# Two items of the first expert worked on inside the attention's schedule, in an adaLN block with a dense-gated mixture of experts

## The chip, the cores and the metric

The kernel runs on one core of a Trainium2 chip. The core has five engines with instruction queues of their own: TensorE (PE in the profile; its weight loads are PEld), VectorE (DVE), ScalarE (ACT), GpSimd (POOL) and SyncE (SP), and 16 DMA engines that they share. The metric is the device time of one execution in microseconds (us); lower is better. A time is the median of several executions without the profiler.

## The reference

The input `x` is 2 sequences of 2,048 tokens with 256 features, in float32. The block is an attention half and an expert half, each with a layer norm, a scale, a shift and a gate that come from a conditioning vector:

```python
h = _layernorm(x) * (1 + ca) + sa
x = x + ga * attention(h)          # 2 heads of 128, one shared key and value head, rope, causal
h = _layernorm(x) * (1 + cb) + sb
gate = softmax(h @ Wg + bg)        # 8 experts
w = relu(gate - 0.125 * sigmoid(h @ Wt + bt)); w = w / (sum(w) or 1)
x = x + gb * sum_e w[:, e] * (gelu(h @ W1[e] + b1[e]) @ W2[e] + b2[e])
```

An expert has a weight above zero for only a part of the tokens, and the kernel computes it for those alone. From the reference's inputs expert 0 has 2,640 of the 4,096 tokens, experts 1 to 7 have 2,609, 2,370, 2,710, 2,418, 2,886, 3,614 and 1,806.

## The kernel before, in words

**The attention half** is a list of steps that a small planner (`Plan`, L40) puts in order when the program is built. Each step has an engine, an assumed cost, the steps it follows, the buffers it takes and gives (`room`, L184), a `late` time for what still has to land, and a rank. At every moment a free engine takes the ready step of lowest rank; the instructions are then emitted in that order, so that an engine's queue is fixed and an instruction that waits holds all behind it. The waits themselves come from the data. Work goes by tiles of 128 tokens (`tile_steps`, L398): load, norm, q, k and v, scores (L498), exponentials (L524), transposes of the probabilities (`turn_p`, L568), `pav` (L580), projection (`proj`, L615), residual, the second norm (`hx`, L638), a copy of its 16-bit halves to `feats` in DRAM (L648), transposes (`turn_h`, L662) and the gate's logits (L671). For groups of tiles `gate_steps` (L689) computes the weights and, for each token and expert, the place in that expert's list; `scatter` (L778) writes the entries of expert 0 to `lists[0]` in DRAM, one indirect DMA for a tile. An entry holds two weights (one per sequence, one of them zero), and the token's number. The tiles of the two sequences alternate; 24 of the 32 tiles come in groups of four, the last four one by one. `total` (L810) writes the counts that the expert half's loops read.

**The expert half** (`experts`, L832) is one critical section with a program for each engine, loops over run-time counts and semaphores by hand. An item is 256 tokens of one expert, in two columns of 128. SP reads an expert's list into `sheets[e]` (L887); POOL copies the item's token numbers (L1100), gathers their rows of `feats` into `xr` by two indirect DMAs (L1055), SP transposes `xr` into `xp` (L895), DVE joins the halves into `xT` (L994), PE does `h = W1 xT` and `y = W2 g` (L944, L935), ACT the gelu between (L970), DVE the bias and the gate (L1025, L1037), and POOL adds the two columns to `out` by two indirect DMAs (L1089). During expert e's first items POOL also writes the list of expert e+1, four tiles with each item (`write`, L1065). If an expert's last item holds at most 128 tokens, it is worked on as one column in a branch of its own (L869).

In the order of time between the halves: the last scatter of expert 0's list lands; all engines pass the barrier of the critical section; SP reads the list (`read(0)`, L903); POOL fetches item 0 (L1119), clears `yo`, writes the first four tiles of list 1 (L1125) and adds zeros to `out` (L1127), since the loop's `add` lies two items behind its fetch; DVE joins `xT` and PE begins. At the end POOL adds the last item's two columns (`add(t0 + 1)`, L1162); where that item has one column, the second one is zeros.

Of the kernel before, what the change touches and what calls it, by code (L numbers as in the profile page):

```python
# [1 line left out]

# [9 lines left out]
F32 = mybir.dt.float32  # L12
BF16 = mybir.dt.bfloat16
I32 = mybir.dt.int32
# [6 lines left out]
P = 128  # L21
# [10 lines left out]
NW = 4  # L32
NP = NTOK // P // NW
SC = 512
EPS = 1e-5
# [63 lines left out]
def adaln_block_kernel(ctx, tc, x, wqkvT, woT, wgt, bgt, w1, b1T, w2, b2, cT, wmod, rope, out):  # L99
# [17 lines left out]


    nc = tc.nc
    PSUM = bass.MemoryType.PSUM  # L120
# [7 lines left out]

    counts = const.tile([P, 3 * E], I32, name="counts")

# [7 lines left out]
    weights = []  # L138

    with tc.manual_schedule():  # L140
        attention(
            tc, x, wqkvT, woT, wgt, bgt, w1, b1T, w2, b2, cT, wmod, rope, out, ident, counts,
            b1_sb, b2_bc, gb_bc, lists, feats, place, entry, weights, wpool,
        )

# [3 lines left out]
    for e in range(RES, E):  # L149
# [4 lines left out]
    xp = ep.tile([P, CI * 2 * KD, P], U16, name="xp")  # L154
    xT = ep.tile([P, KD, TI], F32, name="xT")
    gs = [ep.tile([P, TI], F32, name=f"g{z}") for z in range(4)]
    gate = ep.tile([P, CI, D], F32, name="gate")
    part = ep.tile([P, CI, D], F32, name="part")
    yb = ep.tile([P, CI, D], F32, name="yb")
    yo = ep.tile([P, CI, D], F32, name="yo")  # L160
    sheets = [ep.tile([P, NTOK // P, ENT], F32, name=f"sheet_{e}") for e in range(E)]
    at = ep.tile([P, CI], I32, name="at")
    mcur = ep.tile([P, CI, ENT], F32, name="mcur")
    who = ep.tile([P, CI], I32, name="who")
    to = ep.tile([P, NW], I32, name="to")
# [4 lines left out]
        tc, nc, lists, feats, out.rearrange("b t d -> (b t) d"), counts, ident, b1_sb, b2_bc,  # L170
        gb_bc, w1, w2, weights, xr, xp, xT, gs, gate, part, yb, yo, sheets, at, mcur, who, to, new, place,
        entry, hs, ys,
    )


def attention(
    tc, x, wqkvT, woT, wgt, bgt, w1, b1T, w2, b2, cT, wmod, rope, out, ident, counts,
    b1_sb, b2_bc, gb_bc, lists, feats, place, entry, weights, wpool,
):

    nc = tc.nc
    PSUM = bass.MemoryType.PSUM
    ctx = ExitStack()
    room = {"ps": 6, "pav": 2, "x": 9, "s": 18, "pT": 3, "hx": 4, "hp": 3, "qT": 3, "big": 3, "xn": 3,  # L184
            "hT": 2, "hT2": 2, "aT": 2, "g_sb": 1, "sign": 1, "size": 1, "ga": 1}
# [26 lines left out]

    back = const.tile([P, 2, NTOK // P], F32, name="back")
    limits = const.tile([P, NP], F32, name="limits")
    wqkv_sb = const.tile([P, KD, 4 * HS], F32, name="wqkv_sb")
# [24 lines left out]
    )  # L240
    nc.vector.tensor_copy(back[:, 0, :], ids)
    nc.gpsimd.memset(entry, 0.0)
    nc.gpsimd.tensor_copy(
# [5 lines left out]
    def load(dst, src, kb, rank=first, **how):  # L249
# [13 lines left out]
        for q in range(NT // 4)  # L263
    ]
    l_m1 = load(wm_1, wm[:, :, 2 * D :], 1024, rank=0.5)
    l_wo = load(wo_sb, woT.rearrange("(h p) d -> p h d", p=P), 256, rank=0.5)
    l_wg = load(wgt_sb, wgt.rearrange("(k p) e -> p k e", p=P), 9, rank=0.5)
    l_bg = load(bgt_sb, bgt.partition_broadcast(P), 5, rank=0.5)
    load(b1_sb, b1T, 32, rank=6.0)
    load(  # L270
        b2_bc.rearrange("p e d -> p (e d)"), b2.rearrange("e d -> (e d)").partition_broadcast(P),
# [91 lines left out]

    prev = []
    for e in range(RES):
        prev = [
            plan.add(
                "SP", 11.0, lambda e=e: load_expert(e), after=m_wo + m_mod + [m_T] + prev, late=2.0,
                rank=8.0 + 4 * e,
            )  # L370
        ]


# [24 lines left out]
    def tile_steps(b, i, r, group, g):  # L398
# [161 lines left out]
        def dens():  # L560
            st["rd"] = little([P, NH], "rd", u)
            nc.vector.reduce_sum(st["rd"], st["den"][:, :, :nch], axis=AX.X)
            nc.vector.reciprocal(st["rd"], st["rd"])

        n_d = add("DVE", 0.32, dens, list(n_e.values()))

# [122 lines left out]
    def gate_steps(b, i0, m, q, group, after):  # L689
# [30 lines left out]
        def weigh():  # L720
            st["before"] = before = little([P, 4, E], "before", u, BF16)
            if befores:
                nc.vector.tensor_copy(before[:, 0, :], befores[-1])
            else:
                nc.vector.memset(before[:, 0, :], 0.0)
            befores.append(little([P, E], "next", u, BF16))
            ge, thr = st["ge"][:, :m], st["thr"][:, :m]
            tot = little([P, 4], "tot", u)[:, :m]
            nc.vector.reduce_sum(tot, ge, axis=AX.X)
            nc.vector.reciprocal(tot, tot)  # L730
            nc.vector.tensor_tensor(ge, ge, wide(tot), ALU.mult)
            nc.vector.tensor_scalar(thr, thr, 0.0625, 0.0625, ALU.mult, ALU.add)
            nc.vector.tensor_tensor(ge, ge, wide(thr), ALU.subtract)


            st["on"] = on = little([P, 4, E], "on", u, BF16)
            nc.vector.tensor_scalar(on[:, :m], ge, 0.0, None, ALU.is_gt)
            for j in range(m):
                dst = st["before"][:, j + 1, :] if j + 1 < m else befores[-1]
                nc.vector.tensor_tensor(dst, st["before"][:, j, :], on[:, j, :], ALU.add)  # L740
# [52 lines left out]
        for j in range(m):  # L793
            plan.add(
                "POOL", 1.27, lambda j=j: scatter(j), after=[n], rank=r + 10.0, late=3.0
            )
        return n

    order_w = []
    groups = [(0, 4), (1, 4)] * 3 + [(0, 2), (1, 2), (0, 1), (1, 1), (0, 1), (1, 1)]  # L800
    begun, q = [0] * B, 0
    for b, m in groups:
# [4 lines left out]
        begun[b] += m  # L807
        q += m

    def total():  # L810
# [3 lines left out]
        nc.vector.tensor_copy(n[:, 1:], pn[:, 1:E])  # L814
        nc.vector.tensor_scalar(n[:, :1], pn[:, :1], 1.0, None, ALU.max)
        nc.vector.tensor_copy(counts[:, :E], n)

        more = little([P, E, NP], "more", "")
        nc.vector.tensor_tensor(
# [4 lines left out]
        nc.vector.tensor_copy(counts[:, E : 2 * E], n)  # L824
        nc.vector.tensor_scalar(counts[:, 2 * E :], n, -1.0, float(NP), ALU.mult, ALU.add)

    plan.add("PE", 0.2, total, after=[last], take=["ps"], give=["ps"], rank=q)
    plan.run()
# [3 lines left out]
def experts(  # L832
    tc, nc, lists, feats, rows, counts, ident, b1_sb, b2_bc, gb_bc, w1, w2, weights, xr, xp, xT, gs,
    gate, part, yb, yo, sheets, at, mcur, who, to, new, place, entry, hs, ys,
):
# [3 lines left out]
    LAG = 2  # L839
    ENGINES = (ET.PE, ET.Activation, ET.DVE, ET.Pool, ET.SP)  # L840

# [13 lines left out]
    def items_of(eng, n):  # L855
        return eng.snap((n + (TI - 1)) >> 8, min_val=0, max_val=NTOK // TI)

    def items(eng, n, body, begin=None):
# [16 lines left out]
    with tc.tile_critical():  # L875
# [7 lines left out]
        with nc.Block() as block:  # L883

            @block.sync
            def _(sync):
                def read(e):  # L887

                    if e > 0:
                        sync.wait_ge(sem["written"], (e * NP + 1) * (16 * NW))  # L890
                    sync.dma_start(
# [3 lines left out]
                def turn(t):  # L895

                    sync.wait_ge(sem["loaded"], t * (16 * CI) + 16 * CI)
                    sync.sem_inc(sem["paused"], 1)
# [3 lines left out]

                read(0)  # L903
                turn(0)
                done, t0 = 1, 0
# [57 lines left out]
            def _(act):  # L963
# [11 lines left out]
                def begin(e):  # L975

                    if e == 0:

                        act.wait_ge(sem["planed"], 16)
                    if e + RES < E:  # L980
# [12 lines left out]
            def _(dve):  # L993
# [10 lines left out]
                def item(e, i, t, parts):  # L1004
                    dve.tensor_copy(mcur, sheets[e][:, ds(i * CI, CI), :]).then_inc(
                        sem["copied"], 1
# [34 lines left out]
                def begin(e):  # L1041
                    dve.wait_ge(sem["read"], 16 * e + 16)

                n = [count(dve, e, NTOK) for e in range(E)]
                dve.sem_inc(sem["ready"], 1)
                ready(0)
                items(dve, n, item, begin)

            @block.gpsimd
            def _(pool):  # L1050
# [34 lines left out]

                def scatter(t):

                    for c in range(CI):
                        pool.indirect_dma_start(  # L1089
# [8 lines left out]
                def fetch(index, t):  # L1098
# [3 lines left out]
                    ).then_inc(sem["indexed"], 1)  # L1102
                    wait("indexed", t + 1)
                    gather(t)

                def add(t):
                    wait("added", t * (16 * CI))
                    wait("biased", t + 1)
                    scatter(t)

                def item(e, i, t, also=None):
                    wait("planed", t * 16)
                    fetch(sheets[e][:, ds(i * CI, CI), 2:3], t)
                    if also is not None:
                        also()
                    add(t)

                wait("read", 16)
                fetch(sheets[0][:, 0:CI, 2:3], 0)  # L1119
                pool.memset(yo, 0.0).then_inc(sem["biased"], 1)  # L1120
                pool.iota(
                    who, pattern=[[P, CI]], base=0, channel_multiplier=1
                ).then_inc(sem["biased"], 1)
                wait("biased", 2)
                write(1, 0, 0)  # L1125
                wait("planed", 16)
                scatter(0)  # L1127
                done, t0 = 1, 0
                for e in range(E):
                    many = items_of(pool, count(pool, e, NTOK))  # L1130
                    if e > 0:
                        wait("read", 16 * e + 16)
                    if e == E - 1:
# [27 lines left out]
                add(t0)  # L1161
                add(t0 + 1)  # L1162

# [49 lines left out]
```

## Time and profile before

| what | us |
|---|---|
| median of 3 executions without the profiler (1703.48 to 1704.22) | 1704.15 |
| the profiled execution, its own time | 1719.86 |
| its span, first to last instruction | 1718.0 |
| PE busy in the span (95%) | 1635.1 |
| of it the items' matmuls, L944 and L935 | 675.1 and 673.5 |
| POOL busy (50%) | 863.9 |
| DVE busy (39%), ACT busy (40%) | 678.2, 684.3 |

The profile is of one execution, which is 15.7 us above the median; differences of instants are read from it. PE executes two instructions for each float32 matmul of the code, so an item of 16 + 16 matmuls shows 64 instructions; the 2,816 of L944 are 88 items. Busy time of an engine is not a bound by itself: whether an idle stretch of PE costs time depends on where it lies.

### The profile page before, as it was taken

Reading aid. Unit: us, or ns where it says so; the run is one execution under the profiler, and the core shown is the slowest. Engines: PE = TensorE matmul, PEld = TensorE weight load, DVE = VectorE, ACT = ScalarE, POOL = GpSimd, SP = SyncE. Lnnn points to the kernel's source line nnn. Section 1 sums busy time; section 2 is a strip of 40 time slices with the busy share of each in tenths; the row PEclk is TensorE's granted clock in tenths of the full one; section 3 lists DMA queues with packets and bytes.
Section 4 is the critical chain, followed back from the end, with each engine's and each line's share of the span. In section 5 each row is a group of like instructions: output and inputs, shape, how many; then the busy total and the mean of one; then the engine's idle time right before and its main releaser. Section 6 shows DMA issues by size and latency. Waiting matters only on the chain.

```text
span 1718.0 us, 26912 instructions
## 1 busy us (share of the span) xinstructions
PE 1635.1 (95%) x7665; PEld 1355.1 (79%) x7665; DVE 678.2 (39%) x2215; ACT 684.3 (40%) x1475; POOL 863.9 (50%) x1000
## 2 busy tenths in 40 slices
PE   6999999999949999999999999999999999999996
PEld 3666666677638888888888888888788888888885
DVE  5876766655632332223222232232222232222322
ACT  2444555555523333333333333333333343333432
POOL 2332222111127767765775774676677467744443
PEclk9999999999979999999999999999999999999998
DMA  6210100000014334334434533433433333333333
GB/s 224 84 38 26 35 22 26 25 14 13 16 26 106 59 69 105 59 65 81 85 57 61 105 59 66 99 62 57 104 60 59 61 56 61 60 58 58 64 58 47
DMA packets 166476, 106.98 MB, mean 62 GB/s; under 512 B 110928, under 2 KB 157776, under 8 KB 166288
## 3 DMA queue, kind: packets, MB, share of 16 engines
q0 software_dynamic: 42784, 47.50, 17.4%
q1 hardware_dynamic: 115760, 46.21, 11.6%
q10 hardware_dynamic: 7872, 12.58, 2.3%
q8 instruction: 25, 0.41, 0.1%
q14 instruction: 35, 0.29, 0.1%
HBM read 50.38 MB, written 32.51 MB: 48 GB/s over the span
## 4 chain that ended last, share of the span: by engine, by line
PE 89%; DVE 5%; DMA 2%; issue 1%; POOL 1%; ACT 1%; POOLq 0%; SPq 0%; DVEq 0%; ACTq 0%
PE h L944 34%; PE y L935 34%; PE pav L584 6%; PE psc L502 5%; PE pq L446 3%; PE ptr L574 3%; DMA list<-entry,place 1%; PE po L618 1%; DVE s L513 1%; PE pl L674 1%; PE pr L486 1%; PE ph L665 0%; DVE hx L643 0%; DVE x L625 0%; DVE t L462 0%
## 5 line engine op out<-in xcount | busy, mean ns | idle before, releaser
L944 PE MATMUL h<-xT,w 128*128 128x256 f32 (+1 forms) x2816 | 675.1, 373 | 17.5 <-DVE xT L1001 17.4
L935 PE MATMUL y<-w,g 128*128 128x256 f32 x2704 | 673.5, 380 | 10.8 <-ACT g L970 8.6
L970 ACT ACTIVATE g<-h,b_sb 128x256 f32<-128x256 f32 (+1 forms) x704 | 326.3, 466 | 736.0 <-PE h L944 663.8
L944 PEld LDWEIGHTS h<-xT,w 128*128 128x128 f32 x2816 | 527.1, 191 | 89.0 <-DVE xT L1001 18.6
L935 PEld LDWEIGHTS y<-w,g 128*128 128x128 f32 x2704 | 511.1, 190 | 81.9 <-ACT g L970 9.3
L1089 POOL DMA_INDIRECT out<-yo,who x180 | 295.1, 1639 | 239.1 <-DVE yo L1037 186.4
L1001 DVE COPY xT<-xp 128x512 uint16<-128x512 uint16 x178 | 72.3, 448 | 686.8 <-PE h L944 601.0
L1079 POOL DMA_INDIRECT list<-new,to x228 | 235.2, 1032 | 99.3 <-issue 68.3
L1058 POOL DMA_INDIRECT xr<-feats,at x178 | 179.9, 1011 | 103.3 <-POOL at L1100 74.8
L584 PE MATMUL pav<-pT,v 128*128 128x256 f32 x544 | 145.1, 390 | 0.5 <-ACT pT L578 0.5
L502 PE MATMUL psc<-kT,qT 128*128 128x512 f32 (+3 forms) x320 | 144.2, 537 | 0.7 <-DVE s L513 0.3
L970 ACT ACT_TABLE_LOAD x88 | 112.9, 1283 | 32.2 <-issue 19.6
L513 DVE TENSOR_SCALAR_CACHE_REDUCE s<-psc 128x512 f32<-128x512 f32 (+3 forms) x160 | 95.4, 604 | 74.9 <-PE psc L502 56.1
L529 ACT ACTIVATE s<-s,nmx 128x512 f32<-128x512 f32 (+3 forms) x160 | 103.8, 651 | 50.3 <-DVE nmx L520 50.0
L1025 DVE TENSOR_TENSOR yb<-y,b_bc 128x256 f32<-128x256 f32 x169 | 64.2, 420 | 137.0 <-PE y L935 135.4
L584 PEld LDWEIGHTS pav<-pT,v 128*128 128x128 f32 x544 | 96.3, 193 | 26.1 <-issue 16.0
L578 ACT COPY pT<-ptr 128x512 f32<-128x512 f32 (+1 forms) x144 | 77.0, 563 | 48.8 <-PE ptr L574 29.6
L392 POOL TENSOR_SCALAR rstdf<-mvf 128x1 f32<-128x1 f32 x32 | 8.7, 271 | 162.7 <-DVE mvf L388 92.7
L779 POOL DMA_INDIRECT list<-entry,place x32 | 33.3, 1042 | 106.0 <-DVE place L776 73.7
L574 PEld LDWEIGHTS ptr<-ident,s 128*128 128x128 f32 x544 | 65.4, 144 | 17.3 <-issue 5.3
L1016 DVE SCALAR_TENSOR_TENSOR gate<-gb_bc,mcur,part 128x256 f32<-128x256 f32 x176 | 77.8, 483 | 3.1
L574 PE MATMUL ptr<-ident,s 128*128 128x128 f32 x544 | 76.2, 277 | 2.3 <-ACT s L529 2.1
(132 smaller groups left out, 1054.3 us busy)
## 6 DMA issues: line engine op xcount, KB each, us to landing
w<-in_w ACTq DMA_DIRECT2D x12, 1024.0 KB
x<-in_x SPq DMA_DIRECT2D x32, 128.0 KB, 2.1
out<-x SPq DMA_DIRECT2D x32, 128.0 KB, 1.7
w<-in_w SPq DMA_DIRECT2D x4, 1024.0 KB, 9.0
feats<-hp SPq DMA_DIRECT2D x32, 128.0 KB, 1.7
list<-new,to POOLq DMA_INDIRECT x228
out<-yo,who POOLq DMA_INDIRECT x180
xr<-feats,at POOLq DMA_INDIRECT x178
```

The lines of the kernel that those rows point to most:

```text
L502: nc.tensor.matmul(ps[:, :w], st["qT"][:, h, :], kT[:, ds(c * SC, w)], start=True, stop=not last)
L513: nc.vector.tensor_scalar(s[:, :w], st["sc", h, c][:, :w], 1.0, None, ALU.mult, ALU.max, accum_out=st["mx", h][:, c : c + 1],)
L529: nc.scalar.activation(s[:, :w], s[:, :w], AF.Exp, bias=st["nmx", h], accum_out=st["den"][:, h, c : c + 1],)
L574: nc.tensor.transpose(ptr[:, j, h, :], s[:, ds((c0 + j) * P % SC, P)], ident)
L584: nc.tensor.matmul(st["pav"][:, : NH * P], v[:, c0 + j, :], st["pT", c0][:, j].rearrange("p h t -> p (h t)"), start=(c0 + j == 0), stop=(c ...
L935: last = pe.matmul(ys[c], gs[f % 4][:, ts(c, P)], weights[e][1][:, f, :], start=(f == 0), stop=(f == NF - 1),)
L944: last = pe.matmul(hs[f % 4][:, :w], weights[e][0][:, k, ts(f, P)], xT[:, k, :w], start=(k == 0), stop=(k == KD - 1),)
L970: act.activation(gs[f % 4][:, :w], hs[f % 4][:, :w], AF.Gelu_apprx_tanh, bias=b1_sb[:, at : at + 1],).then_inc(sem["act"], 1)
L1016: last = dve.scalar_tensor_tensor(gate[:, c, :], gb_bc[:, 1, :], mcur[:, c, 1:2], part[:, c, :], ALU.mult, ALU.add,)
L1058: pool.indirect_dma_start(out=xr[:, ts(c, 2 * D)], out_offset=None, in_=feats, in_offset=bass.IndirectOffsetOnAxis(ap=at[:, c : c + 1], ax ...
L1079: pool.indirect_dma_start(out=lists[e], out_offset=bass.IndirectOffsetOnAxis(ap=to[:, j : j + 1], axis=0), in_=new[:, j, :], in_offset=Non ...
L1089: pool.indirect_dma_start(out=rows, out_offset=bass.IndirectOffsetOnAxis(ap=who[:, c : c + 1], axis=0), in_=yo[:, c, :], in_offset=None, b ...
```

## The change

Expert 0's first two items (512 tokens) are worked on in the attention's plan, as steps of rank 1000, which the planner places only where an engine has nothing else ready. For it:

- After the scatters of the first 24 tiles, SP reads the first four columns of expert 0's list into `front`. PE and DVE make `flag`, 1 where these tiles hold at least 512 tokens of expert 0, else 0. With 0 the weights are zero and the two items are done again later. (These 24 tiles hold 1,970.)
- For each of the two items: gather, transpose and join as in the expert half; four PE steps `first`, four ACT steps of two gelus, four PE steps `second`, and DVE steps for the gate and the result, kept in `yo[0]` and `yo[1]`. The PE steps are made to follow the last tile's exponentials.
- After all scatters, the whole list is read, and the third item (or the first, by the flag) is gathered, transposed and joined into `xT`, also in the plan.
- `total` follows the flag, and takes 512 off expert 0's count. `room["s"]` goes from 18 buffers to 16.
- In the expert half the fetch of the first item goes; POOL begins with adding `yo[0]`'s two columns, then the first part of list 1; the first add in the loop is `yo[1]`. Every engine's first waits go; DVE and POOL load one count more.
- At the end POOL adds one column where the last item has one.

```diff
-    room = {"ps": 6, "pav": 2, "x": 9, "s": 18, "pT": 3, "hx": 4, "hp": 3, "qT": 3, "big": 3, "xn": 3,
+    room = {"ps": 6, "pav": 2, "x": 9, "s": 16, "pT": 3, "hx": 4, "hp": 3, "qT": 3, "big": 3, "xn": 3,
...
+    nc.gpsimd.memset(kept.front, 0.0)
     nc.gpsimd.memset(entry, 0.0)
...
+    load(sheet_of_0[:, : AHEAD * CI, :], kept.front, 8, rank=0.7)
...
+        if q == AHEAD_TILES:
+            listed_ahead = list(listed)
+            def filled(group=group):
+                pf = ps_tile("pf")
+                nc.tensor.matmul(pf[:, :1], ones, group["sum"][:, :1], start=True, stop=True)
+                nc.vector.tensor_scalar(flag, pf[:, :1], float(AHEAD * TI), None, ALU.is_ge)
+            n_flag = plan.add("PE", 0.2, filled, after=[last], take=["ps"], give=["ps"], rank=q)
...
+    def low(eng, cost, do, after=(), **how):
+        return plan.add(eng, cost, do, after=after, rank=1000.0, **how)
+    def fetch(index, u, after, to, take=()):
...
+        n = low("POOL", 2.6, gather, after, late=3.0, take=["g_sb"])
+        n = low("SP", 0.1, turn, [n], late=3.5, take=["sign"], give=["g_sb"])
+        return low("DVE", 0.8, join, [n], take=take, give=["sign"])
...
+    n_front = low("SP", 0.1, read_front, listed_ahead + last_score, late=2.5)
...
+    n_w = low("DVE", 0.5, weights_ahead, [n_front, n_flag])
+    before_gelu = list(last_exp)
+    for k in range(AHEAD):
...
+        n_x = fetch(
+            lambda c, k=k: kept.front[:, k * CI + c, 2:3].bitcast(I32), f"_{k}",
+            [n_w], columns, take=["s"],
+        )
...
+        n_g = low("DVE", 1.7, gates, [n_w] + m_wo, take=["size"])
...
+        n_a = []
+        for f0 in range(0, NF, 2):
+            n = low(
+                "PE", 1.74, lambda f0=f0, first=first: first(f0), [n_x, l_first[0]] + before_gelu,
+                take=["ps"], give=["s"] if f0 == NF - 2 else [],
+            )
+            n_a.append(low(
+                "ACT", 1.0, lambda f0=f0, act=act: act(f0), [n, l_b1] + before_gelu + n_a[-1:],
+                take=["s"], give=["ps"],
+            ))
+        n = None
+        for c in range(CI):
+            for f0 in (0, NF // 2):
+                n = low(
+                    "PE", 1.74, lambda c=c, f0=f0, second=second: second(c, f0),
+                    n_a + ([n] if n is not None else []),
...
+        low("DVE", 1.5, result, [n, n_g, l_b2], give=["ps", "size"])
+    n_s = low(
+        "SP", 0.1, lambda: nc.sync.dma_start(kept.sheet, sheet_of_0), listed, late=2.0
+    )
...
+    n = low("DVE", 0.4, behind, [n_s, n_flag])
+    fetch(lambda c: next_at[:, c : c + 1], "_next", [n], lambda: kept.xT)
+    plan.add("PE", 0.2, total, after=[last, n_flag], take=["ps"], give=["ps"], rank=q)
...
-                read(0)
-                turn(0)
+                sync.sem_inc(sem["planed"], 16)
...
                 n = [count(dve, e, NTOK) for e in range(E)]
-                dve.sem_inc(sem["ready"], 1)
-                ready(0)
+                skip = count(dve, 3 * E, AHEAD * CI)
+                dve.sem_inc(sem["ready"], 2)
...
-                wait("read", 16)
-                fetch(sheets[0][:, 0:CI, 2:3], 0)
-                pool.memset(yo, 0.0).then_inc(sem["biased"], 1)
...
+                for k in range(AHEAD - 1):
+                    for c in range(CI):
+                        pool.indirect_dma_start(
+                            out=rows,
...
+                            in_=kept.yo[k][:, c, :],
...
                 write(1, 0, 0)
-                wait("planed", 16)
-                scatter(0)
+                skip = count(pool, 3 * E, AHEAD * CI)
...
                 add(t0)
-                add(t0 + 1)
+                single = pool.snap(
+                    ((count(pool, E - 1, NTOK) + (P - 1)) >> 7) & 1, min_val=0, max_val=1
+                )
+                with pool.If(single > 0):
+                    add(t0 + 1, 1)
+                with pool.If(single < 1):
+                    add(t0 + 1)
```

A `first` step is two of the eight blocks of 128 hidden features times two halves of the input, for 256 tokens; a `second` step is four blocks for one column of 128 tokens; each is four matmuls of 256 columns in the code, eight PE instructions. `act` is two gelus of 128x256. `gates` is four DVE instructions of 128x256, `result` three and a small copy.

## The prediction, made before the change was run

> **What bounds the kernel now.** I read the page's slices first, then its chain of waits, then the end of the attention in windows and in the chain.
>
> ```profile
> PE   6999999999949999999999999999999999999996
> PE 89%; DVE 5%; DMA 2%; issue 1%; POOL 1%; ACT 1%; POOLq 0%; SPq 0%; DVEq 0%; ACTq 0%
> ```
>
> The first line is PE's busy share in 40 slices of 43 us; the second is the chain's share by engine. PE is the bound nearly everywhere, with one hole in the twelfth slice. An item's matmuls repeat every 13.81 us without a gap, so an item taken out of the expert half is worth 13.81 us, provided that its work goes where PE now stands still. The windows around the hole (length, then busy us and instructions of PE, PEld, DVE, ACT and POOL, then clock, DMA share, GB/s):
>
> ```profile
> 480.00:490.00 10.00, 8.19 (x41) 6.61 (x39) 1.85 (x7) 3.30 (x6) 1.09 (x1) 1.00 0.01 2
> 490.00:500.00 10.00, 2.10 (x9) 1.46 (x9) 5.66 (x34) 0.67 (x3) 2.69 (x4) 0.57 0.08 26
> 500.00:510.00 10.00, 0.00 (x0) 0.00 (x0) 0.00 (x0) 0.00 (x0) 3.53 (x9) 0.50 0.12 34
> ```
>
> PE is idle for 1.8 + 7.9 + 10.0, and 4.2 more until 514.17: **23.9 us**. Two items need 2 x 13.81 = **27.6 us**. So the hole is almost as large as the work, and the question is what ends it. The chain says (start, length, what):
>
> ```profile
> 497.39 0.17 DVE entry L750
> ...
> 499.01 2.29 DMA list<-entry,place
> ...
> 502.41 1.90 DMA sheet<-list
> ...
> 506.82 2.77 DMA xr<-feats,at
> ...
> 509.77 3.42 DMA xp<-xr
> ...
> 514.17 5.12 PE h L944 x12
> ```
>
> The last tile's projection (ends 488.65), norm, transposes (492.90), logits (494.4), gate and count (496.5) lead to the scatter at 499.01, list read, gather, transpose and join at 514.12. The change keeps all these, for the third item's columns, but puts 16 PE steps of eight instructions (1.73 us each) beside them. PE's queue is fixed, so a chain step now stands behind whichever low step was put before it.
>
> **The tail, step by step.** The front read goes out behind the store at 470.5 and lands about 473 (the list read took 1.90). The weights, three DVE instructions of 0.17, come after the logits of tile 30: 476.4. Gather 4.1 (505.51 to 509.59), transpose 3.5, join 0.8: item 0 can start on PE at **485.3**, where the trace has the fifth or sixth `pav` of the last tile. The second gather needs the first one's buffer, so it runs 484.7 to 488.8, its transpose to 492.6.
>
> Working the planner's rule through with the costs in the code gives this PE order: first, pav, first, pav, first, proj, first, first (item 1), second, turn_h, second, logits, second, first, count, second, first, total, first, four seconds. With the trace's durations, a low step at 1.73 and the ends before beside it:
>
> - last `pav` 490.7 (was 487.1), behind two low steps and a wait of 0.3: +3.6
> - `proj` 493.5 (488.65), behind one more: +4.9
> - transposes 499.3 (492.9): the second join, 0.8, stands before the norm on DVE, and three low steps on PE: +6.4
> - logits 502.0 (494.4): +7.6; count 505.7 (496.5): +9.2; scatter 506.9 (499.0): +7.9, since the 1.1 us of `spread` now run while the count waits
> - list landed and read (2.29, 0.1, 1.90): 511.3. DVE meanwhile has item 0's result (1.5), item 1's gate (1.7) and `total`'s small ones (1.2), from 507.5 to 511.9; the index takes 0.4 and then gather 4.1, transpose 3.6 and join 0.9 end at **521.2** (514.1): +7.1
>
> PE's low work itself ends at 519.0. So the chain, not PE, still ends the tail, by 2 us.
>
> **What was hidden comes out.** The engines passed the barrier 1.1 us after the scatter landed (501.32 to 502.41), then loaded their counts and entered their loops under the fetch. Now barrier, loads and loop entry come after the join with nothing beside them. DVE loads nine counts before it lets PE start. The trace shows no load. The nearest rows: POOL's three loads and loop entries between experts 0 and 1 add nothing to its step from scatter to copy (659.83 to 660.85, against 543.42 to 544.45 inside the loop), so they cost under 0.3 each; DVE's loop entry took 1.0 (514.12 to 515.12). The Trainium skill (DMA: Bandwidth & Descriptors, Latency and other measured facts) speaks against the change: a `tensor_load` has a floor of about 600 ns. By it nine loads and the entry are an estimated 6.4 us; by the rows, at 0.18, 2.6. I take the rows, 2.6, and keep 1.0 to 6.4. PE starts at 521.2 + 1.1 + 2.6 = **524.9, 10.8 later** than now.
>
> The clock: PE stopped at 488.65, and the granted clock (last but two in each row) fell within 3 us, came back only at 518.6, and cost the first item 2.2 us (16.0 instead of 13.81).
>
> ```profile
> 490.00:491.00 1.00, 0.00 (x0) 1.00 0.38 129
> 491.00:492.00 1.00, 0.00 (x0) 0.73 0.01 2
> 517.00:518.00 1.00, 1.00 (x4) 0.50 1.00 406
> 519.00:520.00 1.00, 1.00 (x7) 1.00 1.09 363
> ```
>
> With PE idle from 519.0 to 524.9 it falls again, so I book these 2.2 us as unchanged; a gap under 3 us would save them. ACT's tables switch exp, gelu, exp, gelu instead of once: 1.28 each in the trace; the Trainium skill (ScalarE: Activation LUTs, What ACT_TABLE_LOAD costs) adds a drain, 2.66 together. Only the switch before the last gate's exp is in the chain, and ACT is free for 2.8 us there: nothing by either, up to 2.7 without that cover.
>
> **POOL in the expert half.** POOL's steps to fetch an item begin with this copy; the last row is SP's read of list 1:
>
> ```profile
> 518.37 0.33 POOL L1100 COPY at<-sheet 128x2 int32 x1
> 531.23 0.77 POOL L1100 COPY at<-sheet 128x2 int32 x1
> 611.96 0.77 POOL L1100 COPY at<-sheet 128x2 int32 x1
> 623.30 0.35 SPq L891 DMA_DIRECT2D sheet<-list  x1
> ```
>
> From copy to transposed columns is 8.3 (518.37 to 526.7), join 0.9. POOL's loop takes 93.6/7 = 13.37, just under PE's 13.81. After the change POOL first adds two columns (3.5), writes a part of list 1 (6.3) and loads counts (0.5): the next item's copy comes 10.3 after the barrier, 7.7 after PE's start (before: 4.2). Its columns are there at +16.9, the first item ends at +16.0: **0.9 lost** (0 to 3). POOL gains 0.44 an item, so no more is lost inside expert 0. But expert 0's loop with writes takes nine items, and nine are all that is left (2,640 - 512 = 2,128 tokens); before, two items without writes followed. List 1 is read 11.3 after the ninth item's copy, and POOL reaches expert 1's first copy at +115.2 from PE's start; the columns are there at +124.4. PE has done the ninth item, a half one of 9.3, at +122.9: **1.5 lost** (0 to 4), where the trace now loses 0.2.
>
> **The end.** The last two scatters start at 1707.01 and 1708.88. Expert 7's 1,806 tokens make 15 columns, so one is left out: **1.9 gained** (0.5 to 2); the count and the branches lie under the wait for the result. Costs at nothing: the memset and the 8 KB store at the start (in 16 busy DMA engines, 0.1); two buffers fewer of `s`, since two late tiles take 16, and PE waits only 1.0 us from 330 to 470 (without that cover some 2); the flag.
>
> **Sum.** 27.6 - 10.8 - 0.9 - 1.5 + 1.9 = 16.3 us. The profiled execution's 1719.9 would become 1703.6, its span 1701.7; the median is 15.7 below that execution, and I take the difference over: **1688 us**.
>
> **Rivals.**
>
> - *The tail is delayed less.* Each of five chain steps waits half a low step, 4 us in all instead of 7: the join is done at 518. Then PE's end, 519.0, and item 1's result (1.5 on DVE) set the barrier at 520.5; with loads and entry at 1.0 PE starts at 522.6, 2.3 earlier than in my sum; the gap of 3.6 may keep the clock (2.2), and POOL may lose nothing (2.4): 6.9 more, 1681. For it: the low steps are short. Against: all three have to come together.
> - *Slower: a low matmul waits at the head of PE's queue.* The first `first` stands before two `pav`s of the last tile; if its columns are late, everything behind stands, microsecond for microsecond. The fetch has three DMAs in series, and the second item's is chained to the first by its buffer and stands before `turn_h`. It decides from 16 us late on the two together; a fetch that waits for the last stores to `feats` or list entries would be some 20 late: 1708. For it: each landing costs 2 to 3.4 us and the placement rests on assumed times. Against: everything the first fetch needs is there by 476.6.
> - *It does not do what it says.* With the flag 0 nothing comes off and the two items are done twice: 1704 + 11 = 1715. The inputs give 1,970 against 512 wanted.
> - *Nothing to see*: loads at 6.4, instruction fetches on the jumps (the half item shows 1.7 of PE waiting there), a transpose held by earlier DMAs (2.3) and two more low steps (3.5) take 11.3 of the 16.3: 1699, or with POOL's stalls at their upper ends 1703.
>
> **Chances.** My sum with the first rival 0.80, the slower queue 0.09, flag 0.02, the last rival with its upper part 0.09, of which 0.04 is within 0.2% (3.4 us, about what a measurement can tell from no change) and 0.05 still faster. Faster 0.85, same 0.04, slower 0.11. The range 1680 to 1699 holds the first case and the lower part of the last.
>
> **What would show it.** Right: PE's hole at 490 to 510 filled at clock 1.0; `xT` ready near 521 and the first item of the loop near 525; 2,752 instructions of L944; one scatter at the end. Wrong: PE waiting in front of a `first` or `pav` before 490, PE's start after 530, POOL as releaser of PE in expert 0.

## The result, and the profile after

| | median, us | range, us | executions |
|---|---|---|---|
| before | 1703.62 | 1702.83 to 1704.22 | 6 |
| after | 1695.95 | 1694.8 to 1698.32 | 6 |

The ratio is 0.9957, with a 95% interval of 0.9947 to 0.9967: **7.7 us faster**, where 16 were forecast (1688, range 1680 to 1699). The direction was right, and the time lies in the range; but more than half of the expected gain is missing, and the rest of this text is about where it went. The profiled execution of after took 1694.8 us, with a span of 1693.0.

From the page of after, the busy share of PE in 40 slices of 42.3 us and the group of the items' first matmuls (busy us and mean ns of one, then PE's idle time just before them and what ended most of it):

```profile
PE   6898999999998997999999999999999999999997
L1142 PE MATMUL h<-xT,w 128*128 128x256 f32 (+1 forms) x2752 | 659.8, 373 | 16.3 <-DVE xT L1196 9.0
```

The 4 of the twelfth slice is now a 9; what is left of the hole is the 8 of the thirteenth (508 to 550 us), where PE waits for the loop to begin. A new hole, a 7, has come in the sixteenth slice (635 to 677 us). L1142 has 2,752 instructions, 64 fewer, as forecast. Its idle time names the new hole: 9.0 us in which PE waited for `xT`. The windows of the tail in after (length, busy us and instructions of PE, PEld, DVE, ACT, POOL, then clock, DMA share, GB/s):

```profile
490.00:500.00 10.00, 9.80 (x49) 8.43 (x48) 4.10 (x12) 5.14 (x11) 1.83 (x3) 1.00 0.26 66
500.00:510.00 10.00, 10.00 (x50) 8.66 (x49) 5.66 (x34) 3.26 (x7) 1.10 (x1) 1.00 0.03 8
510.00:520.00 10.00, 8.77 (x41) 7.40 (x39) 3.00 (x9) 1.68 (x4) 1.93 (x2) 1.00 0.23 52
520.00:530.00 10.00, 3.89 (x9) 3.17 (x10) 2.70 (x9) 0.55 (x2) 5.61 (x7) 0.66 0.50 130
```

Where before had 2.1 and 0.0 us of matmuls, PE is now full, at clock 1.0. So the tail did what was expected of it. The new hole is at the switch from expert 0 to expert 1. The chain of waits that ended last runs through POOL's steps and its fetches during all of expert 0. At the switch it reads (start, length, what):

```profile
641.16 0.20 POOL at L1296
...
643.52 2.75 DMA xr<-feats,at
...
646.50 7.34 DMA xp<-xr
...
654.74 5.24 PE h L1142 x12
```

PE had ended the half item of expert 0 at 645.76. POOL's copy for expert 1's first item is at 641.16, the gather lands at 646.3, and SP's transposes take 7.34 us, more than twice the 3.42 of the tail before. What else was asked for then is in the timeline of after (start, length of the request, queue, line, operation):

```profile
644.50 0.38 ACTq L1177 DMA_DIRECT2D w<-in_w  x1
644.92 0.50 ACTq L1180 DMA_DIRECT2D w<-in_w  x1
646.50 1.35 SPq L1100 DMA_TRANSPOSE xp<-xr  x1
```

When ACT ends expert 0, it asks for the weights of expert 3, two transfers of 1 MB, 2 us before the transposes start. And PE stood long enough for its clock to fall (windows of 1 us of after):

```profile
648.00:649.00 1.00, 0.00 (x0) 0.00 (x0) 0.00 (x0) 0.00 (x0) 0.69 (x2) 1.00 0.96 386
649.00:650.00 1.00, 0.00 (x0) 0.00 (x0) 0.00 (x0) 0.00 (x0) 0.69 (x2) 0.68 0.92 281
650.00:651.00 1.00, 0.00 (x0) 0.00 (x0) 0.00 (x0) 0.00 (x0) 0.70 (x2) 0.50 1.09 361
659.00:660.00 1.00, 1.00 (x4) 0.79 (x4) 0.43 (x2) 0.03 (x1) 0.88 (x1) 0.70 0.10 37
```

The clock column shows the mean of a window: 0.68 is full clock for the first third and half clock behind it, so it fell at 649.4, 3.6 us after PE stopped. The 0.70 of the last row puts its return at 659.6, 4.9 us after PE started again. So expert 1's first item takes 16.3 us instead of 13.81.

### The profile page after: what moved, and what is told of

Read it like the earlier page. It is cut to its first block, busy times and chain, and to the rows that moved or that the text cites. A ratio compares the mean times of both kernels' runs of the same rounds, so it can differ in the third digit from the quotient of the medians.

```text
span 1693.0 us, 26695 instructions
## 1 busy us (share of the span) xinstructions
PE 1627.9 (96%) x7666; PEld 1354.3 (80%) x7666; DVE 677.9 (40%) x2220; ACT 575.1 (34%) x1390; POOL 855.9 (51%) x991
## 4 chain that ended last, share of the span: by engine, by line
PE 60%; DMA 3%; POOL 2%; issue 2%; POOLq 0%; DVE 0%; SPq 0%; DVEq 0%
PE h L1142 30%; PE y L1133 30%; DMA xp<-xr 2%; POOL out L1285 1%; DMA xr<-feats,at 1%; POOL list L1275 0%; DMA out<-yo,who 0%; POOL xr L1254 0%; POOLq L1035 0%; POOL out L1317 0%; POOL at L1296 0%; POOLq L1083 0%; POOLq L1296 0%; DVE yo L1232 0%; DVE xT L896 0%
## 5 line engine op out<-in xcount | busy, mean ns | idle before, releaser
L1142 PE MATMUL h<-xT,w 128*128 128x256 f32 (+1 forms) x2752 | 659.8, 373 | 16.3 <-DVE xT L1196 9.0
L1133 PE MATMUL y<-w,g 128*128 128x256 f32 x2640 | 654.2, 379 | 0.0
L1168 ACT ACTIVATE g<-h,b_sb 128x256 f32<-128x256 f32 (+1 forms) x688 | 319.6, 465 | 847.5 <-PE h L1142 844.8
L1142 PEld LDWEIGHTS h<-xT,w 128*128 128x128 f32 x2752 | 515.6, 192 | 85.4 <-DVE xT L1196 10.5
L1133 PEld LDWEIGHTS y<-w,g 128*128 128x128 f32 x2640 | 499.2, 190 | 65.2
L1285 POOL DMA_INDIRECT out<-yo,who x173 | 283.0, 1636 | 212.8 <-DVE yo L1232 160.6
L1196 DVE COPY xT<-xp 128x512 uint16<-128x512 uint16 x172 | 68.4, 439 | 613.9 <-PE h L1142 581.2
L1254 POOL DMA_INDIRECT xr<-feats,at x172 | 173.7, 1010 | 100.9 <-POOL at L1296 70.2
L528 PEld LDWEIGHTS psc<-kT,qT 128*128 128x128 f32 x320 | 56.9, 191 | 15.3 <-issue 6.2
```

Of the source, the lines that this page charges most:

```text
L528: nc.tensor.matmul(ps[:, :w], st["qT"][:, h, :], kT[:, ds(c * SC, w)], start=True, stop=not last)
L1133: last = pe.matmul(ys[c], gs[f % 4][:, ts(c, P)], weights[e][1][:, f, :], start=(f == 0), stop=(f == NF - 1),)
L1142: last = pe.matmul(hs[f % 4][:, :w], weights[e][0][:, k, ts(f, P)], xT[:, k, :w], start=(k == 0), stop=(k == KD - 1),)
L1168: act.activation(gs[f % 4][:, :w], hs[f % 4][:, :w], AF.Gelu_apprx_tanh, bias=b1_sb[:, at : at + 1],).then_inc(sem["act"], 1)
L1254: pool.indirect_dma_start(out=xr[:, ts(c, 2 * D)], out_offset=None, in_=feats, in_offset=bass.IndirectOffsetOnAxis(ap=at[:, c : c + 1], ax ...
L1285: pool.indirect_dma_start(out=rows, out_offset=bass.IndirectOffsetOnAxis(ap=who[:, c : c + 1], axis=0), in_=yo[:, c, :], in_offset=None, b ...
```

## Experiments

The theory to test, A: POOL comes late to expert 1, because the items without list writes, its slack, have left the loop, and PE's wait of 9.0 us with the 2.5 us of clock behind it is the missing gain. Rivals: the wait is made by the meeting of expert 3's weights with the transposes; or the gain is misread elsewhere, in ACT's table loads, which vanished from the loop, or in the end. The runs fell on four chips, the first four kernels on one, so each ratio is to the kernel before on the same chip. Instants are compared in profiled executions, one for each run.

**The kernel before, once more.**

> The kernel before, once more. The profile that the prediction used is of an execution 15.7 us above the median; its seven half items (128 tokens) took 9.1 to 9.4 us, the changed kernel's 7.0. If the seven half items are the excess (7 x 2.3 = 16), another execution shows them at 7.0, PE's first item still near 514, and a span near 1702. If the excess is spread over all items, they show 9 again with items longer elsewhere, or the items' period is not 13.81.

It took 1701.44 us, with a span of 1699.6. PE's waits in the expert half, first in the profile that the forecast was made from, then in this one (total us, times, longest):

```profile
PE h L944 <- DVE xT L1001: 17.4, 1, 17.4
PE y L935 <- ACT g L970: 8.6, 10, 1.7
PE y L935 <- issue: 2.2, 3, 1.0
```

```profile
PE h L944 <- DVE xT L1001: 17.2, 1, 17.2
```

In the second one PE waits for nothing behind its first item. The half item of expert 0 took 7.03 us in it, and the others at most 7.26. In the first profile that item took 9.1, and four of the six others 8.0 to 12.1, the last two 7.0 and 7.2 (not all seven 9.1 to 9.4, as the expectation had it). From PE's first item to its last end the loops differ by 18.0 us, and some 15 of them are in the half items. So the forecast's 9.3 us for a half item is not a price that holds in every execution: on this chip and the next the profiles show 7.0 to 7.5, and on the third and fourth chip, below, long half items come back.

**Expert 3's weights later.** ACT asks for them with those of expert 4, at the begin of expert 2:

```diff
-                    if e + RES < E:
-                        w1_e, w2_e = weights[e + RES]
+                    for x in {0: (2,), 1: (), 2: (3, 4), 3: (5,), 4: (6,), 5: (7,)}.get(e, ()):
+                        w1_e, w2_e = weights[x]
```

> The changed kernel; the 2 MB of expert 3's weights are asked for when expert 2 begins, not expert 1. Theory A (POOL has no slack left when expert 0 ends, and the transpose of expert 1's first item then meets these 2 MB): the transpose takes 3.4 instead of 7.3, PE's wait before expert 1 goes from 9.0 to about 5.2, the clock still falls, total 3.5 to 4.5 us less (1691.5 to 1692.5). Rival B (the meeting alone makes the wait): the wait nearly goes, 9 to 11 us less (1685 to 1687). Rival C (the wait is POOL's alone, the transfer merely fills the time): no difference within 1 us.

1695.7 us, ratio 0.9960 (0.9947 to 0.9974). The chain at the switch, in this kernel:

```profile
638.83 0.20 POOL at L1296
...
644.28 3.34 DMA xp<-xr
...
648.48 4.34 PE h L1142 x12
```

The transposes are back at 3.34 us and PE's wait is down from 9.0 to 4.0, but not gone; 1.1 of the difference is POOL's copy, which came that much earlier after PE's start. The item behind the wait took 15.4 us, so the switch costs 5.7 us instead of 11.6. A new wait of 2.2 us stands before expert 2's second item, where 4 MB now start together and the transposes take 8.33; it costs 3.2 us. The time can't be told from the change's, and the 3.5 to 4.5 us less that theory A expected are not shown. So the meeting is real and costs some 4 us at this place; without it POOL is still late.

**A gelu before the loop**, in the kernel before, behind the last gate, so that the loop finds its table loaded:

```diff
+    plan.add(
+        "ACT", 0.3,
+        lambda: nc.scalar.activation(dot, neg_half, AF.Gelu_apprx_tanh), after=[last], rank=2000.0,
+    )
```

> The kernel before with one gelu of 128x1 after the last gate, so that ACT's loops need no table load of their own (before: one 1.28 us load with each of 88 items; the changed kernel shows none). If the loads lie beside PE's work everywhere: no difference within 1 us. If they stand in the path of the seven half items or of the first: 1 to 9 us less, and that part of the change's gain has nothing to do with the work ahead.

1703.38 us, ratio 1.0004 (0.9996 to 1.0012). The 88 table loads of 1.28 us in the loop are gone from the trace, as they are in after, and ACT is busy 573.6 us instead of 684.8; the time is the same, and so is the loop, 1171.9 us against 1171.4. The 109 us that ACT lost in after are worth nothing: they were hidden.

**Both columns at the end**, in after:

```diff
-                with pool.If(single > 0):
-                    add(t0 + 1, 1)
-                with pool.If(single < 1):
-                    add(t0 + 1)
+                add(t0 + 1)
```

> The changed kernel with both columns added at the end again. The end is 1.9 us later (1.6 to 2.1), as between the starts of the two scatters, so 1697.9. If the last landing is covered by the drain anyway: under 0.5.

1698.76 us, ratio 0.9974 (0.9967 to 0.9981). From the last matmul's end to the end of the span it is 14.4 us, in before (the second profile) 14.6, in after 12.2. The scatter left out is worth 2.1 to 2.3 us.

**The changed kernel again, on a second chip**, beside the next two kernels.

> The changed kernel again, to stand beside the next two on the same chip: 1695 to 1697, PE's wait before expert 1's first item 9 us in the trace.

1696.94 us, ratio 0.9965 (0.9952 to 0.9979). PE starts the loop at 527.12, waits 8.9 us before expert 1, and the loop takes 1154.9 us from PE's first item to its last end, as in after (1154.6).

**List 1 written in the attention's plan**, so that POOL writes nothing during expert 0 (core of the edit; POOL's loop for expert 0 and SP's reads follow it):

```diff
+        for j in range(m):
+            plan.add("POOL", 1.27, lambda j=j: scatter(j, 1), after=[n], rank=r + 10.5, late=3.0)
...
-                write(1, 0, 0)
```

> The changed kernel, with expert 1's list written in the attention's plan too (32 more indirect DMAs of POOL there), so that POOL writes no list during expert 0 and is not 10 us behind at its end. Theory A (POOL without slack at the end of expert 0): the wait of 9.0 before expert 1 and the slow clock after it (2.2 to 2.6) go, 10 to 12 us less than the changed kernel: 1684 to 1686. Rival B (the meeting with expert 3's weights makes the wait): the fetch may be early but the wait stays over 3 us; 0 to 5 less. If the extra scatters get in the way of the norm's steps on POOL, PE's first item comes later than 527 and a part is given back.

1698.8 us, ratio 0.9970 (0.9958 to 0.9982). PE's waits in its expert half:

```profile
PE h L1151 <- DVEq L1037: 7.0, 1, 7.0
PE h L1151 <- DVE xT L1205: 0.7, 1, 0.7
```

The wait before expert 1 is 0.7 us, and the loop takes 1144.7 us, **10.2 less** than in the changed kernel on the same chip. But PE's first item of the loop starts at 540.51 instead of 527.12: the 32 added scatters lengthen the attention by 13.4. With POOL early the wait and its clock go. ACT asks for the weights at the same point of its program, but the transposes now start at 657.55, 2.0 us ahead of that (659.51), and take an undisturbed 3.07: POOL's lateness and the meeting go together. As a version it gains nothing; the 1684 to 1686 expected are missed by what the added scatters cost.

**One item ahead instead of two**, so that the loop of expert 0 has one more item:

```diff
-AHEAD = 2
+AHEAD = 1
...
-                            in_=kept.yo[k][:, c, :],
+                            in_=kept.nil,
```

> The changed kernel with one item worked on ahead instead of two. Expert 0 then has ten items, one of them without list writing, in which POOL regains some 6.4 us. Theory A: no wait before expert 1 (at most 1), the same time as with two items ahead: 13.8 more work in the loop, 11.4 less of wait and slow clock, PE's first item some 3 earlier (523): 1694 to 1697. Rival D (the wait belongs to expert 0's shorter run in any form, or to the switch of experts): the wait stays at 5 or more, 1701 to 1706.

1703.23 us, ratio 0.9997 (0.9986 to 1.0007): a time that the rival in the expectation had, but with the wait before expert 1 gone, as theory A has it. The span of its profiled execution is 4.8 us longer than that of the changed kernel beside it. The ledger of both: PE starts 5.0 earlier; one more item, 13.8; the switch to expert 1 costs 0.3 instead of 11.6; the other half items 1.5 more; 5.8 more in full items, nearly all at the switch from expert 3 to 4. The first row is PE's waits, the second is from the page:

```profile
PE h L1144 <- issue: 22.6, 4, 18.2
L1170 ACT ACT_TABLE_LOAD x87 | 111.6, 1283 | 33.6 <-issue 21.3
```

Of these waits 18.2 lie ahead of the loop's first item and 4.0 lies at that later switch, where the profile names nothing that PE waits for. Why it comes there is open. The edit also did one thing more than intended: here the last function that ACT uses ahead of the loop is the gate's exp again, and 87 table loads are back in the loop. In the kernel before, 88 of them cost nothing.

**Expert 3's weights asked earlier**, before the half item instead of behind it, on a third chip where the kernel before took 1720.95 us:

```diff
+                def mid(e):
+                    fill(e + RES + 1)
...
-                items(act, [count(act, e, NTOK) for e in range(E)], item, begin)
+                items(act, [count(act, e, NTOK) for e in range(E)], item, begin, mid)
```

> The changed kernel; ACT asks for each later expert's weights before the half item of the expert before, some 9 us earlier than now, so that expert 3's 2 MB have passed when expert 1's first transpose starts, and nothing is put elsewhere twice. Theory A (two causes: POOL late, and the meeting): the transpose takes 3.4 instead of 7.3, PE's wait before expert 1 is 5 instead of 9, still with a slow clock after it: 3 to 5 less than the changed kernel, 0.993 to 0.995 of the kernel before. Rival B (meeting alone): the wait is under 1, 10 to 12 less. Rival C: no difference.

1715.66 us, ratio 0.9972 (0.9961 to 0.9984). The chain of this kernel:

```profile
636.72 6.90 DMA sheet<-list
...
645.08 0.20 POOL at L1304
...
650.84 3.28 DMA xp<-xr
...
655.07 4.41 PE h L1144 x12
```

The transposes take 3.28, but the weights are now asked for at 635.93, the 64 KB read of list 1 behind them takes 6.90 (1.90 in the tail before), and POOL waits for it. The bulk transfer only met an earlier link of the same chain: PE's wait is 9.0 us again, not the 5 that theory A expected, and the half item with the first item of expert 1 still takes 11.5 us more than their undisturbed time.

**The first part of list 1 written once.** In after, POOL writes it ahead of the loop and again in it. Here the loop writes the seven others, and is done with the list one item sooner:

```diff
-                        wait("written", w * (16 * NW) + 16 * NW)
-                        w = w + 1
+                        wait("written", w * (16 * NW))
...
+                        if e == 0:
+                            a = pool.snap((a * (NP - 1) + (NP - 1)) >> 3, min_val=0, max_val=NP - 1)
+                            front = pool.snap((front * (NP - 1)) >> 3, min_val=0, max_val=NP - 1)
...
-                            write(e + 1, nc.s_assert_within(c, 0, NP - 1,
+                            c = c + done
+                            write(e + 1, nc.s_assert_within(c, done, NP - 1,
```

> The changed kernel, but POOL does not write the first part of list 1 twice (once ahead of the loop, again with the first item), so the last of expert 0's items has no part to write: POOL is 6.3 us earlier at expert 1's first fetch, its gather lands before the weights are asked for, its transpose takes 3.4. Theory A: PE's wait before expert 1 goes (under 1) and the clock stays: 10 to 12 less than the changed kernel, 1684 to 1686 or 0.989 to 0.991 of the kernel before; PE's first item stays at 525 to 527. Rival C' (the wait is bound to the switch, not to POOL's lateness): it stays over 4, 0 to 6 less.

On the third chip 1709.1 us, ratio 0.9931 (0.9916 to 0.9946), where 0.989 to 0.991 were expected; the changed kernel itself was not run on this chip. PE doesn't wait for `xT` before expert 1: the half item, 9.0 us long here, starts at 640.58, expert 1's first item at 649.64, and that item is at full clock. The transposes, started at 643.98, are out of the way of the weights, which ACT asks for at 648.46.

**Both of these edits together.**

> Both edits. By theory A the meeting is gone already with the first one, so the same as with the part written once, within 1.5 us. If the half items of other experts meet the earlier transfers, up to 3 more.

1711.36 us, ratio 0.9940 (0.9927 to 0.9954), which can't be told from the version above. The wait is back, at 3.4 us: the weights are now asked for at 638.33, just behind POOL's copy (637.55), and the transposes start 8.8 us after that copy, not 5.7 as in the version above. So here the weights meet the gather.

**The changed kernel and the list part written once, side by side on a fourth chip**, where the kernel before took 1728.83 us.

> The changed kernel once more, on one chip with the version that writes the first part of expert 1's list once. Theory A (POOL late at the switch of experts) and the rival (the meeting of transfers) both expect what it showed before: a ratio to the kernel before of about 0.9960, PE's wait before expert 1 of 6 to 9 us by how long the half item is on this chip, and the item behind it some 2.5 us long through the clock.

> As the changed kernel, but the loop of expert 0 doesn't write the first part of list 1 a second time (eight writes in place of nine). Theory A: no wait for xT before expert 1 over 1 us and expert 1's first item at full clock, so 9 to 12 us less than the changed kernel on the same chip, a ratio to the kernel before of about 0.990. The rival: the weights still start beside the transposes, so 3 us less at most, a ratio of 0.994 or more.

The changed kernel took 1718.0 us, ratio 0.9949 (0.9934 to 0.9964), the other one 1719.32, ratio 0.9947 (0.9929 to 0.9965). The expected 9 to 12 us are not there. PE's waits in the loop, of the changed kernel and of the other one:

```profile
PE h L1142 <- DVE xT L1196: 8.8, 1, 8.8
PE y L1133 <- ACT g L1168: 7.4, 6, 2.4
PE y L1133 <- issue: 4.8, 3, 2.1
```

```profile
PE y L1135 <- ACT g L1170: 11.1, 7, 2.5
PE y L1135 <- issue: 6.1, 7, 2.0
```

The wait for `xT` is gone again, as theory A expects, and with its clock the switch costs 10.0 us less. But the half items of experts 1, 2, 4 and 5 took 12.2 to 12.4 us instead of 10.6 to 11.4, together 6.0 more, and scattered full items, of 14 to 15.4 us, 4.3 more. These are one execution each, but the medians agree that nothing is left of the gain. What makes these items longer is open. And in both runs of this version the half item of expert 0 was long, 9.0 and 8.5 us, and ended together with the join (649.6 and 648.2); with 7.0 us of cover part of the wait could have stayed. So this version beats the kernel before on both chips, and is not shown to beat the change.

## Why the prediction was right in direction and wrong in size

Between the profiled executions of after and of the kernel before once more (6.6 us apart, 1694.8 and 1701.44), the terms are as follows, in us (whether both ran on one chip isn't known):

| term of the sum | forecast | measured |
|---|---|---|
| two items off the loop | -27.6 | -27.6 |
| PE starts the loop later | +10.8 | +12.4 (526.11 against 513.69) |
| first item of the loop | +0.9 | -0.4 |
| switch to expert 1 | +1.5 | +11.6 (wait with half item 9.1, clock 2.5) |
| half items of the other experts | 0 | -0.3 |
| end | -1.9 | -2.3 |
| sum | -16.3 | -6.6 |

**The step that failed** is the ninth item: "PE has done the ninth item, a half one of 9.3, at +122.9: 1.5 lost (0 to 4)". Counted from PE's start, POOL's copy for expert 1 came at +115.05, where the forecast had +115.2; that half of the step was right to 0.2 us. Three things around it were not. PE was done at +119.65, 3.3 earlier, of which 2.3 are the half item, 7.03 and not 9.3: cover that the first profile promised and this execution didn't have. The columns were there at +128.6, 4.2 later, of which 3.9 are the transposes beside expert 3's weights; the forecast took their price from a place where nothing else moved. And the clock, which the forecast booked for the gap in the tail, was put at nothing here, without a reason; it cost 2.5. So 1.5 became 11.6: 10.1 us, about the 9.7 by which these two executions fall short of the 16.3.

What removes the wait is shown twice at half items of 7.2 us: POOL writing nothing during expert 0, and one more item in the loop. With one part less to write it was gone as well, but beside longer half items. With the weights moved later the switch still cost 5.7 of its 11.6 us; with the weights moved earlier, all of it. So POOL's lateness opens the wait, and the meeting, which comes only because POOL is late, about doubles its cost. That the whole kernel gains what the switch loses is not shown: each version that had no wait lost as much elsewhere, or wasn't run beside the changed kernel.

**The tail** went as worked out. The last `pav` ended at 490.7 (forecast 490.7), the projection at 493.3 (493.5). From there the planner's order was kinder: logits at 499.4 (502.0), count 503.0 (505.7), scatter 504.1 (506.9). The chain lost that lead again on DVE, whose rows in after are (start, length, line):

```profile
508.45 0.76 DVE L971 TENSOR_TENSOR yo<-pya,b_bc 128x256 f32<-128x256 f32 x2 [0.47 <-PE pya L964]
...
511.14 0.48 DVE L937 SCALAR_TENSOR_TENSOR size_a<-gb_bc,wts_a,size_a 128x256 f32<-128x256 f32 x1
511.54 0.15 DVE L1009 TENSOR_TENSOR next_at<-sheet 128x2 int32<-128x2 int32 x1
...
520.27 0.76 DVE L896 COPY xT<-sign_p_next 128x512 uint16<-128x512 uint16 x2
```

The list was asked for at 506.60, but the index (L1009) stood behind item 0's result and item 1's gate until 511.54; the forecast had 511.9. The join ended at 521.0, forecast 521.2, and PE's low work at 518.8, forecast 519.0. The first rival, a chain delayed less, was half true up to the scatter and brought nothing.

**Barrier, counts and loop entry** took 5.1 us from the join to PE's start (521.0 to 526.1), where the sum had 1.1 + 2.6. Without the barrier, taken at its 1.1 as before, an estimated 4.0 lie between the 2.6 by the rows and the 6.4 by the floor for a `tensor_load` that the Trainium skill states (DMA: Bandwidth & Descriptors, Latency and other measured facts): the rows that I took were too kind by 1.4, the page's figure would have been too dear by 2.4. The clock's fall there, 2.0 us on the first item, was as before.

**The rest**: the table switches cost nothing, as booked; POOL held nobody inside expert 0, where 0.9 was booked, since PE started later and the copy came at +6.1 instead of +7.7; the scatter left out was worth 2.1 to 2.3 for 1.9. No rival happened as a whole. PE idled only 0.3 us before its first low step, the flag was 1, and the time lies below the 1699 of the last rival. But two parts of that rival came: loads above the rows' price (1.4 of its 3.8), and transposes held by other transfers, 3.9 us, at the switch, instead of 2.3.

## What to carry to other kernels

Items taken off the front of a loop take with them the slack of the slower engine that rides beside it: list for every engine which iterations are its slack, and what it still has to do in those that are left. Price cover from more than one execution, and by the shortest: a row of a long one can promise cover that isn't there. A wait can cost more than its length: here 0.7 us of wait before expert 1 left the next item at 13.9 us, and waits of 3.4 to 9.4 left it 1.6 to 2.6 longer than 13.8. And a transfer that moves must be priced beside what runs where it lands.

## What the runs showed of the hardware

- An item's DMA transposes, 3.4 us in the tail before, took 7.3, and a list read of 1.9 took 6.9, beside a 2 MB load of weights. With the load moved away the transposes were back at 3.3.
- The same half item took 7.0 us in some executions and 9 to 12 in others, with PE waiting for ACT or for nothing named. All seven profiled executions on the first two chips have the short ones, 7.0 to 7.5 us without the wait for `xT`. In all five on the third and fourth chip the half items of experts 1, 2, 4 and 5 took 9.9 to 12.4, whatever the kernel, and there the kernel before took 1721 and 1729 us instead of 1703. The half items of experts 6 and 7 took 7.0 to 7.5 in every profile. What sets it is open.
- The table loads of the loop, 1.28 us each and one for every item, are gone in the kernels whose last function ahead of the loop is the gelu (88 to 0), are there where it is the exp (88, and 87 with one item ahead), and their going is worth nothing.
